# The Mamba layer's engines run in the written order, with more states between the steps of a unit's preparation and closing; D x joins TensorE's sum; two norms in a row take one root

## The chip, the cores and the metric

The kernel runs on one core of a Trainium2 chip. The metric is the device time of one execution in microseconds (us). Five executions of the kernel before took 4131.66 to 4149.81 us, with a median of 4142.33. One further view comes from the hardware profiler: it recorded the execution that took 4132.69 us, and every duration below that is not called a median is from that recording. Its span, from the first to the last instruction, is 4130.8 us.

The engines are TensorE (PE; its weight loads are listed apart as PEld), VectorE (DVE), ScalarE (ACT), GpSimd (POOL) and SyncE (SP), which issues the DMAs. Each works through its own list of instructions in order; an instruction that waits holds up all that stand behind it on that engine.

## The reference

The program is a stack of eight layers on 2048 rows of 128 numbers (8 sequences of 256). Each layer has the form `x = x + layernorm(layer(layernorm(x)))`. The change touches the seventh, a pair of Mamba blocks, one forward and one on the flipped sequence:

```python
xn = _layernorm(x, ln1_w, ln1_b)          # x is layernorm(x) of the stack already
x1 = _mamba(xn, m1_...)
x2 = flip(_mamba(flip(xn), m2_...))
return _layernorm(x1 + x2, ln2_w, ln2_b) + xn

def _mamba(x, ...):                        # E = 256 channels, N = 64 states, R = 8
    xp, z = split(x @ W_in.T)
    xc = silu(causal_conv(xp, 4 taps) + conv_b)
    dt_lo, B, C = split(xc @ W_xp.T)
    dt = softplus(dt_lo @ W_dt.T + dt_b)
    h = exp(dt * A) * h + (dt * xc) * B    # scan over time, per channel and state
    y = sum over states of h * C
    y = y + xc * D
    return (y * silu(z)) @ W_out.T
```

So a row is normed twice in a row ahead of the blocks: once by the stack, once by the layer. All numbers are f32. The last layer is a gated MLP; the six before are attention, convolution and expert layers.

## The kernel before

**The first six layers** are written as many small tasks. A planner in the program orders them by estimated costs, and a helper, `as_written` (line 156), ties the instructions of TensorE, VectorE, ScalarE and GpSimd to that order. The change leaves them as they are. The last two layers, `l3_attn` (line 1848) and `l3_ffn`, are not tied: there the order on each engine is chosen when the kernel is built, by a scheduler that goes by its own estimates of readiness and may move an instruction ahead of others written earlier.

**Units and states.** `l3_attn` works in eight units. A unit is one Mamba block (forward or flipped) on two sequences; units 0 and 1 belong to the first group of sequences, 2 and 3 to the second, and so on. A unit has 64 states, and the loop walks over all 512. For state n of a unit:

- `start` (line 2042) has SyncE load the row C of the state, broadcast to 128 partitions (`Cs`, L2046, five buffers), and ScalarE make `dA` = exp(dt A) (L2053, two instructions, three buffers). For even states ScalarE also makes `sT` = dtx B (L2050, four instructions, one per even state).
- `inputs` (line 2056) has TensorE put (dt x) B into PSUM: for even states by eight transposes of `sT` (L2068), for odd ones by 32 small products with `dB` (L2066). `dB` is made by GpSimd for two odd states at a time, three states ahead (`pre`, L2040).
- `scan` (line 2070): VectorE runs the recurrence over time (L2074), then GpSimd multiplies h by C into `hc` (L2076). In every eighth state VectorE makes this product itself, straight from PSUM.
- `add` (line 2078): three states later TensorE adds `hc`, transposed, into the unit's sum `ps_y` in PSUM (L2086, eight transposes).

In iteration i the program writes, in this order: `pre` of i+3, `inputs` of i-1, `start` of i, `scan` of i-1, `add` of i-4, one step of the closing of the unit before, one step of the preparation of the unit after.

**Preparation** (`prologue`, line 1909) starts at state 6 of the unit before. It is a generator; each `yield` is one state's pause. For the first unit of a group it norms x twice (`norm_steps`, line 220, once for each norm in a row), multiplies and adds the weights on GpSimd (L1916, L1917), then for all units: transposes or flips (L1924, L1926), four convolutions as 16 products (L1937) with a ScalarE copy each, the gate (L1944), Silu (L1948), the products for B, C and dt (L1953, L1956, L1967), Softplus (L1970), `dtx` on GpSimd (L1973), its transposes (L1983) and copy. DMAs turn `B` and `dtx` (`Bt`, `dtxTt`, L1906) and write C to memory (`cd`, L1962). If it has not ended by state 60 the rest is written at once.

**Closing** (`epilogue`, line 1988) starts at state 3 of the unit after: ScalarE copies the sum (`yT`, L1992), TensorE transposes it back (L1997), VectorE adds D x (L2001, two instructions), GpSimd multiplies by silu(z) (L2003), TensorE multiplies by W_out (L2009), ScalarE copies (L2012). After the second unit of a group the flip (L2019), the sum of both blocks (L2022), a norm, three GpSimd instructions (L2024 to L2028), a second norm and the addition to x (L2033) follow.

**A norm in steps** (`norm_steps`) is: VectorE statistics (L227, L228), GpSimd a sum and a power -0.5 (L230, L231), then four states later a small VectorE multiply (L234), one state later four ScalarE instructions (L237).

PSUM: three slots of two banks are shared by the inputs of all states (`ps_h`) and every product of preparation and closing (`ps_a`); `ps_y` has its own. A slot is free again when all readers of its tile are done.

Of the kernel before, what the change touches and what calls it, by code (L numbers as in the profile page):

```python
# [17 lines left out]
P = 128  # L18
# [154 lines left out]
class Ctx:  # L173
# [46 lines left out]
    def norm_steps(self, dst, src, n):  # L220
# [9 lines left out]
        nc.gpsimd.tensor_scalar(rs, mv[:, :, 1], EPS, None, ALU.add)  # L230
        nc.gpsimd.tensor_tensor(rs, rs, self.mhalf.to_broadcast([P, n]), ALU.pow)  # L231
        for i in range(4):
            yield
        nc.vector.scalar_tensor_tensor(mv[:, :, 0], mv[:, :, 0], -1.0, rs, ALU.mult, ALU.mult)  # L234
        yield
# [1612 lines left out]
def l3_attn(k):  # L1848
# [17 lines left out]
    with ExitStack() as es:  # L1866
# [10 lines left out]
        for m, w in enumerate(k.l3a):  # L1877
# [8 lines left out]
            nc.vector.tensor_scalar(w["A"], w["A"], 1e-20, -1.0, ALU.max, ALU.mult)  # L1886
        xTs, CLs = [], []
# [21 lines left out]
        def prologue(u, o):  # L1909
            g, m = divmod(u, 2)  # L1910
            w = k.l3a[m]
            if m == 0:
                xs = xns[g] = s2.tile([P, 4, D], F32, name="xn")
                yield from k.norm_steps(xs, k.x[:, 4 * g:4 * g + 4, :], 4)
                yield from k.norm_steps(xs, xs, 4)
                nc.gpsimd.tensor_tensor(xs, xs, over(k.l3a_ln[:, 0, :], 4, 1), ALU.mult)  # L1916
                nc.gpsimd.tensor_tensor(xs, xs, over(k.l3a_ln[:, 1, :], 4, 1), ALU.add)  # L1917
                yield
            xT, CL = xTs[u % 2], CLs[u % 2]
            ps = pb()  # L1920
            for j in range(4):
                d = slice(j * P, (j + 1) * P)
                if m == 0:
                    nc.tensor.transpose(ps[:, 0, d], xns[g][:, j, :], k.ident)  # L1924
                else:
                    nc.tensor.matmul(ps[:, 0, d], xns[g][:, j ^ 1, :], k.flip, start=True, stop=True)  # L1926
            yield
# [5 lines left out]
            for ec in range(2):  # L1933
                for b in range(2):
# [3 lines left out]
                    yield  # L1938
                    nc.scalar.activation(xc[:, ec, b * L:(b + 1) * L], ps[:, 0, 0:L], AF.Identity, bias=w["cols"][:, ec, 0:1])
                    yield  # L1940
                    yield
            for ec in range(2):
                ps = pb()
                nc.tensor.matmul(ps[:, 0, :], w["win"][:, 256 + ec * P:256 + (ec + 1) * P], xT[:, :, 3:3 + L], start=True, stop=True)  # L1944
                yield
# [11 lines left out]
            yield  # L1957
            B = s2.tile([P, 4, N], F32, name="B")
# [10 lines left out]
            yield  # L1969
            nc.scalar.activation(dt, ps, AF.Softplus)  # L1970
# [6 lines left out]
            yield  # L1977
            dtxT = s2.tile([P, 4, 2, P], F32, name="dtxT")
            ps = pb()
            for j in range(4):  # L1980
                for ec in range(2):
                    n = 2 * j + ec
                    nc.tensor.transpose(ps[:, n // 4, n % 4 * P:(n % 4 + 1) * P], dtx[:, ec, j * P:(j + 1) * P], k.ident)  # L1983
            yield
# [3 lines left out]
        def epilogue(u, o):  # L1988
# [4 lines left out]
            yield  # L1993
            py = pb()
# [3 lines left out]
            yield  # L1998
            t = s2.tile([P, 2, U], F32, name="t", tag="sp_u")
            for ec in range(2):  # L2000
                nc.vector.scalar_tensor_tensor(t[:, ec, :], o["xc"][:, ec, :], w["cols"][:, ec, 2:3], py[:, ec, :], ALU.mult, ALU.add)  # L2001
            yield
            nc.gpsimd.tensor_tensor(t, o["sz"], t, ALU.mult)  # L2003
# [236 lines left out]
```

## Time and profile before

| what | value |
|---|---|
| median of five executions | 4142.33 us |
| the profiled execution | 4132.69 us |
| its span | 4130.8 us |
| first scan of the Mamba layer begins | 2695.46 us |
| last product of its loop ends | 4045.9 us |
| VectorE busy from 2690 to 4046 | 1229.39 of 1356 us |
| GpSimd busy in it | 1241.29 us |
| ScalarE busy in it | 1197.18 us |
| TensorE busy in it | 1186.36 us, granted clock 0.98 |
| one scan (L2074) | 2266 ns x448, 2275 ns x64 |
| one hc on GpSimd, on VectorE (L2076) | 2371 ns, 1224 ns |
| one dB (L2040) | 1062 ns |
| one dA, one sT instruction | 715 ns, 495 ns |

An instruction's recorded time overlaps its neighbour's by a little, so a row of equal instructions takes less than their sum: seven scans in a row take 15.34 us. A busy share is an average over stages; which engine sets the pace has to be read stage by stage. A wait is put down to the event that came last.

### The profile page before, as it was taken

The page shows a single profiled execution, that of the slowest core. Times are in us where ns is not written, and L with a number is a line of the kernel's source. Part 1 is how long each engine was busy: PE and PEld are TensorE (multiplying, and loading weights), DVE is VectorE, ACT ScalarE, POOL GpSimd, SP SyncE. Part 2 cuts the span into 40 slices and gives each one's busy share as a digit, 9 for nine tenths or more (in the row PEclk, how much of TensorE's full clock was granted, in tenths as well). Part 3 has the DMA queues.
Part 4 walks back from the last instruction along what each step waited for, and adds up shares of the span by engine and source line. Part 5 has one row for each costly group of instructions (what it writes and reads, how often), then busy time and mean ns, then how long its engine had stood idle before and what let it go on. Part 6 is the DMA issues. An engine that isn't in the chain of part 4 may idle for free. (4 is left out here: it accounts for less than half of the span.)

```text
span 4130.8 us, 125166 instructions
## 1 busy us (share of the span) xinstructions
PE 3574.2 (87%) x55265; PEld 2808.5 (68%) x55265; DVE 3020.0 (73%) x4217; ACT 2525.5 (61%) x4465; POOL 2642.0 (64%) x1991
## 2 busy tenths in 40 slices
PE   6989988999888888999889998688988988898886
PEld 4777777777776565656555555377877876777774
DVE  7677677776755756645575568379979988998995
ACT  4455544545544545545454444299979988998993
POOL 5667667566854544332332333489989988998993
PEclk8999999999999999999999898799999999999997
DMA  1000000000001000000000000033323333443430
GB/s 58 3 3 2 3 2 3 3 2 9 2 19 38 1 1 12 25 12 11 1 1 1 6 1 1 13 110 111 112 80 115 109 106 90 110 111 91 116 114 25
DMA packets 98677, 168.89 MB, mean 41 GB/s; under 512 B 16699, under 2 KB 26582, under 8 KB 98006
## 3 DMA queue, kind: packets, MB, share of 16 engines
q1 hardware_dynamic: 98134, 160.89, 13.7%
q8 instruction: 434, 7.11, 0.7%
q14 instruction: 109, 0.89, 0.1%
HBM read 153.51 MB, written 2.10 MB: 38 GB/s over the span
## 5 line engine op out<-in xcount | busy, mean ns | idle before, releaser
L2076 POOL TENSOR_TENSOR hc<-h,Cs 128x1024 f32<-128x1024 f32 x448 | 1049.5, 2371 | 97.2 <-DVE h L2074 85.2
L2074 DVE TENSOR_TENSOR_SCAN h<-dA,ps_h 128x1024 f32<-128x1024 f32 x448 | 988.9, 2266 | 89.9 <-PE ps_h L2068 53.6
L2053 ACT ACTIVATE dA<-dt,A 128x512 f32<-128x512 f32 x1024 | 684.5, 715 | 125.4 <-DVE h L2074 92.6
L2086 PE MATMUL ps_y<-w_c_ident,hc 128*128 128x128 f32 x4096 | 561.9, 281 | 118.6 <-POOL hc L2076 85.9
L2086 PEld LDWEIGHTS ps_y<-w_c_ident,hc 128*128 128x128 f32 x4096 | 454.3, 143 | 173.1 <-POOL hc L2076 157.4
L2050 ACT ACTIVATE sT<-dtxT,B 128x256 f32<-128x256 f32 x1024 | 449.8, 495 | 3.9 <-PE ps_h L2068 3.9
L590 DVE SCALAR_TENSOR_TENSOR acc<-ps,w_l0a_conv,acc 128x254 f32<-128x254 f32 (+2 forms) x768 | 309.5, 470 | 30.6 <-ACT acc L584 30.4
L2066 PE MATMUL ps_h<-dB,dtxTt 64*64 64x64 f32 x16384 | 301.7, 223 | 19.4 <-DVE h L2074 10.1
L2066 PEld LDWEIGHTS ps_h<-dB,dtxTt 64*64 64x64 f32 x16384 | 265.9, 136 | 73.1 <-issue 46.9
L2068 PE MATMUL ps_h<-w_c_ident,sT 128*128 128x128 f32 x2048 | 276.5, 279 | 19.4 <-DVE h L2074 16.9
L2068 PEld LDWEIGHTS ps_h<-w_c_ident,sT 128*128 128x128 f32 x2048 | 239.6, 145 | 31.5 <-DVE h L2074 23.6
L742 POOL TENSOR_TENSOR Ps<-M,w_c_levels 128x512 f32<-128x512 f32 x192 | 241.9, 1275 | 5.0 <-DVE M L716 4.1
L359 ACT COPY XY<-ps 128x1024 f32<-128x1024 f32 (+1 forms) x128 | 120.5, 945 | 178.0 <-PE ps L807 164.5
L800 PE MATMUL ps<-Z,XY 64*64 64x64 f32 x4608 | 173.4, 226 | 36.0 <-DVE Z L784 25.2
L230 POOL TENSOR_SCALAR ln_rs<-ln_mv 128x4 f32<-128x4 f32 (+1 forms) x84 | 22.0, 262 | 280.2 <-DVE ln_mv L228 253.2
L800 PEld LDWEIGHTS ps<-Z,XY 64*64 64x64 f32 x4608 | 144.4, 137 | 53.2 <-DVE Z L784 27.0
L807 PE MATMUL ps<-XY,Z 64*64 64x64 f32 x5120 | 173.2, 225 | 4.4 <-issue 4.2
L784 DVE TENSOR_TENSOR Z<-ps,w_c_ident 128x512 f32<-128x512 f32 x160 | 108.0, 685 | 71.8 <-PE ps L781 71.0
L1633 ACT ACTIVATE e<-ps,nm 128x256 f32<-128x256 f32 x256 | 99.9, 484 | 99.2 <-DVE nm L1630 83.7
L351 PE MATMUL ps<-ident 128*128 128x512 bf16 x401 | 111.0, 429 | 55.2 <-DVE qn L1077 11.5
L807 PEld LDWEIGHTS ps<-XY,Z 64*64 64x64 f32 x5120 | 151.8, 138 | 7.1 <-issue 7.0
L2074 DVE TENSOR_TENSOR_SCAN ps_h<-dA,ps_h 128x1024 f32<-128x1024 f32 x64 | 145.6, 2275 | 14.8 <-PE ps_h L2066 14.5
(451 smaller groups left out, 8533.7 us busy)
## 6 DMA issues: line engine op xcount, KB each, us to landing
Cs<-cd SPq DMA_DIRECT2D x512, 256.0 KB, 3.3
dtxTt<-dtxT SPq DMA_DIRECT2D x32, 128.0 KB, 3.9
wk<-in_l0a_w SPq DMA_DIRECT2D x8, 256.0 KB, 5.7
w_h<-in_l1f_h SPq DMA_DIRECT2D x4, 512.0 KB, 3.9
w_l2a<-in_l2a_w SPq DMA_DIRECT2D x3, 512.0 KB, 4.1
w_l0a_wg<-in_l0a_wg SPq DMA_DIRECT2D x1, 1024.0 KB
w_qk<-in_l0f_wqkv SPq DMA_DIRECT2D x2, 512.0 KB, 3.9
cv<-in_l3a_m_conv SPq DMA_DIRECT2D x2, 512.0 KB, 5.1
```

Of the source, the lines that this page charges most:

```text
L359: self.nc.scalar.copy(out, in_)
L590: nc.vector.scalar_tensor_tensor(acc[:, n, s:L], p4[:, n, 0:L - s], conv[:, h2, 4 * j + n, 3 - s:4 - s], acc[:, n, s:L], ALU.mult, ALU.add,)
L742: nc.gpsimd.tensor_tensor(t, M[:, :, 0:64], over(k.l0a_levels[:, n, :], 8, 1), ALU.mult)
L800: nc.tensor.matmul(ps[own, a, at(j)], XY[rows, t, at(i)], Z[rows, za, at(zj)], start=True, stop=True)
L807: nc.tensor.matmul(ps[to, a, at(4 + j)], Z[rows, za, at(zj)], XY[rows, t, at(i)], start=True, stop=True)
L2050: nc.scalar.mul(st["s"][:, j], o["dtxT"][:, j], o["B"][:, j, n:n + 1])
L2053: nc.scalar.activation(dA[:, :, ec, :], by_seq(o["dt"][:, ec, :]), AF.Exp, scale=w["A"][:, ec, n:n + 1])
L2066: nc.tensor.matmul(ps[q, b, ec, j * 64:(j + 1) * 64], o["dtxTt"][rows, j, ec, q], dB[rows, j, :], start=True, stop=True)
L2068: nc.tensor.transpose(ps[:, j // 2, ec, j % 2 * P:(j % 2 + 1) * P], st["s"][:, j, ec, :], k.ident)
L2074: nc.vector.tensor_tensor_scan(h.rearrange(flat), st["dA"].rearrange(flat), st["in"].rearrange(flat), 0.0, ALU.mult, ALU.add)
L2076: (nc.vector if on_v else nc.gpsimd).tensor_tensor(st["hc"], h, over(by_seq(st["C"]), 2, 2), ALU.mult)
L2086: nc.tensor.matmul(o["py"][:, 2 * b + j, ec, :], st["hc"][:, b, ec, j * P:(j + 1) * P], k.ident, start=first, stop=n == N - 1, is_transpos ...
```

## The change

- `l3_attn` is wrapped in `as_written` for the four compute engines. SyncE's DMAs are not in it.
- The preparation and the closing get more `yield`s: two states instead of one between a TensorE product and the instruction that takes it out of PSUM, three between VectorE's product t and the output product, four between the layer's norm and its transposes, four instead of two behind `dtx`. `norm_steps` takes the number of pauses as a parameter; this layer uses three ahead of the small multiply and three behind it.
- The two norms in a row become one: the second's variance is v / (v + EPS), so that both together have the root of (1 + EPS) v + EPS².
- D x is summed by TensorE: a diagonal matrix D (128 x 128 per half of the channels) is made ahead of the loop, and eight products of `xc` with it open the sum `ps_y`. The VectorE instructions of L2001 go; the product with silu(z) moves from GpSimd to VectorE, one instruction reading PSUM.

```diff
-    def norm_steps(self, dst, src, n):
+    def norm_steps(self, dst, src, n, twice=False, steps=(4, 1)):
...
-        nc.gpsimd.tensor_scalar(rs, mv[:, :, 1], EPS, None, ALU.add)
+        if twice:
+            nc.gpsimd.tensor_scalar(rs, mv[:, :, 1], 1.0 + EPS, EPS * EPS, ALU.mult, ALU.add)
+        else:
+            nc.gpsimd.tensor_scalar(rs, mv[:, :, 1], EPS, None, ALU.add)
         nc.gpsimd.tensor_tensor(rs, rs, self.mhalf.to_broadcast([P, n]), ALU.pow)
-        for i in range(4):
+        for i in range(steps[0]):
             yield
         nc.vector.scalar_tensor_tensor(mv[:, :, 0], mv[:, :, 0], -1.0, rs, ALU.mult, ALU.mult)
-        yield
+        for i in range(steps[1]):
+            yield
...
+            w["D"] = s1.tile([P, 2, P], F32, name="D", bufs=2)
+            for ec in range(2):
+                nc.vector.tensor_scalar(w["D"][:, ec, :], k.ident, w["cols"][:, ec, 2:3], None, ALU.mult)
...
-                yield from k.norm_steps(xs, k.x[:, 4 * g:4 * g + 4, :], 4)
-                yield from k.norm_steps(xs, xs, 4)
+                yield from k.norm_steps(xs, k.x[:, 4 * g:4 * g + 4, :], 4, True, (3, 3))
                 nc.gpsimd.tensor_tensor(xs, xs, over(k.l3a_ln[:, 0, :], 4, 1), ALU.mult)
                 nc.gpsimd.tensor_tensor(xs, xs, over(k.l3a_ln[:, 1, :], 4, 1), ALU.add)
-                yield
+                for _ in range(4):
+                    yield
...
                         nc.tensor.matmul(ps[:, 0, 0:L], w["wk"][:, tap, ec * P:(ec + 1) * P], xT[:, b, tap:tap + L], start=tap == 0, stop=tap == 3)
                     yield
+                    yield
                     nc.scalar.activation(xc[:, ec, b * L:(b + 1) * L], ps[:, 0, 0:L], AF.Identity, bias=w["cols"][:, ec, 0:1])
                     yield
-                    yield
...
             t = s2.tile([P, 2, U], F32, name="t", tag="sp_u")
-            for ec in range(2):
-                nc.vector.scalar_tensor_tensor(t[:, ec, :], o["xc"][:, ec, :], w["cols"][:, ec, 2:3], py[:, ec, :], ALU.mult, ALU.add)
-            yield
-            nc.gpsimd.tensor_tensor(t, o["sz"], t, ALU.mult)
+            nc.vector.tensor_tensor(t, py, o["sz"], ALU.mult)
+            yield
             yield
             yield
...
-            yield from k.norm_steps(xs, xs, 4)
+            yield from k.norm_steps(xs, xs, 4, steps=(3, 3))
...
-            yield from k.norm_steps(yn, xs, 4)
+            yield from k.norm_steps(yn, xs, 4, steps=(3, 3))
...
             if n == 0:
                 o["py"] = psumy.tile([P, 4, 2, P], F32, name="ps_y")
+                for j in range(4):
+                    for ec in range(2):
+                        nc.tensor.matmul(
+                            o["py"][:, j, ec, :], o["xc"][:, ec, j * P:(j + 1) * P], w["D"][:, ec, :],
+                            start=j % 2 == ec == 0, stop=False, skip_group_check=True,
+                        )
...
-                layer(k)
+                with as_written(tc, COMPUTE if layer is l3_attn else ()):
+                    layer(k)
```

Not shown are the further single `yield`s added behind the other products (the transposes, the gate, B and C, dt, `dtx`, yT, the output product, the flip).

## The prediction

> **What bounds the kernel now.** I read the page's engine totals first, then the mean by stretch, then VectorE's waits over the Mamba layer, and last the timeline where those waits are longest. Columns of the stretches: length, then busy us (instructions) of TensorE, its weight loads, VectorE, ScalarE, GpSimd, then granted clock, DMA share, GB/s.
>
> ```profile
> PE 3574.2 (87%) x55265; PEld 2808.5 (68%) x55265; DVE 3020.0 (73%) x4217; ACT 2525.5 (61%) x4465; POOL 2642.0 (64%) x1991
> 2720.00:2780.00 60.00, 57.36 (x1037) 49.45 (x1035) 52.26 (x25) 57.98 (x106) 53.27 (x27) 1.00 0.36 102
> 3140.00:3200.00 60.00, 51.63 (x1124) 45.70 (x1113) 59.90 (x30) 55.03 (x104) 59.01 (x30) 1.00 0.39 115
> 3040.00:3100.00 60.00, 45.66 (x674) 39.69 (x673) 39.80 (x54) 39.95 (x81) 43.34 (x30) 0.86 0.21 62
> ```
>
> The totals hide three regimes. Where a unit only walks through its states (second stretch) VectorE is busy 59.9 of 60 us: it sets the pace and GpSimd is one step behind. Where the next unit is prepared (first) TensorE and ScalarE are full. Where a group ends (third) nobody is full: a third of the time is waiting.
>
> ```profile
> 2998.03 2.27 DVE L2074 TENSOR_TENSOR_SCAN ps_h<-dA,ps_h 128x1024 f32<-128x1024 f32 x1
> 3003.84 7.03 POOL L2076 TENSOR_TENSOR hc<-h,Cs 128x1024 f32<-128x1024 f32 x3 [0.34 <-DVE h L2074]
> 3010.83 1.05 POOL L2040 TENSOR_TENSOR dB<-w_c_ident,Bt 128x512 f32<-128x512 f32 x1
> 3011.85 9.35 POOL L2076 TENSOR_TENSOR hc<-h,Cs 128x1024 f32<-128x1024 f32 x4
> 3016.74 2.27 DVE L2074 TENSOR_TENSOR_SCAN ps_h<-dA,ps_h 128x1024 f32<-128x1024 f32 x1
> ```
>
> Eight states take 3016.74 - 2998.03 = 18.71 us, 2.339 each; GpSimd idles 0.34 of it. 512 states at this pace are 1197.4 us. Counting scans along the timeline, the eight units begin at 2695.46, 2856.91, 3020.19, 3206.25, 3368.95, 3555.78, 3718.53 and 3893.59, and the last product ends at 4045.9. Over 64 x 2.339 = 149.7 they lose 11.8, 13.6, 36.4, 13.0, 37.2, 13.1, 25.4 and 2.6: 153 us. What the change can win in the layer lies in these.
>
> ```profile
> DVE h L2074 <- PE ps_h L2068: 53.6, 17, 35.8
> DVE ln_mv L234 <- POOL ln_rs L231: 30.4, 10, 3.7
> DVE ln_st L227 <- POOL x L2028: 13.3, 3, 4.4
> DVE t L2001 <- PE ps_a L1997: 6.2, 7, 1.7
> 3055.75 0.16 DVE L234 SCALAR_TENSOR_TENSOR ln_mv<-ln_mv,ln_rs 128x4 f32<-128x4 f32 x1 [3.07 <-POOL ln_rs L231]
> 3062.55 0.29 DVE L227 BATCH_NORM_STATS2 ln_st<-x 128x6 f32<-128x128 f32 x1 [4.44 <-POOL x L2028]
> 3075.30 1.22 DVE L234 SCALAR_TENSOR_TENSOR ln_mv<-ln_mv,ln_rs 128x4 f32<-128x4 f32 x1 [3.72 <-POOL ln_rs L231]
> ```
>
> In the group's end VectorE stands at an instruction of a norm whose input GpSimd has not reached, with the next scan queued behind; without that scan GpSimd, ScalarE and TensorE stop too. (35.8 of the first line is the start of the layer.)
>
> **The change, part by part.**
>
> *Order and spacing.* The layer's four engines now run in the order written. The state loop's own order barely moves; the steps between do. Norm steps get three to four states between engines, and in the built order four or five scans stand between a norm's statistics and the small multiply that needs GpSimd's root. GpSimd may be 5.4 us behind the scan (hc 6 below) plus 1.3 for the root: 6.7 against three scans of 2.19, 6.6. So the waits of 30.4 and 13.3 go, nearly whole. What is late next are the sums. In units 2, 4, 6 (which carry a group's end and the next preparation) between states 4 and 24 TensorE gets D x 1.95, yT 1.0, output product 1.95, flip 1.06, xT 1.06, four convolutions of 1.9 and two gates of 0.95: 16.5 us beside 1.93 per state (3033.82 to 3037.49 and on, four groups in 3.86 for two states). Its room is 20 x (2.34 - 1.93) = 8.2, so 8.3 is lost, which also covers VectorE's own 3.5 (t, sum, statistics). From 24 to 39 ScalarE gets a copy 0.57, Silu 1.9 with two table loads of 1.28, 4.5, two copies 0.9, Softplus with two loads 3.6, a norm 1.65, a copy 1.0: 12.2, against 2.175 per state (3008.15 to 3012.50 for two), room 16 x 0.165 = 2.6 and a lead of 1.4: 8.2. Together 16.5 instead of 36.4, 37.2, 25.4: -49.5. The bounds of this term: 12 per unit as in unit 0, where no group ends (-63); and half of it if the waits only change place (-25).
>
> Units 1, 3, 5 now hold the next group's norm, which stood in units 2 and 4 and before the loop: VectorE 1.5, GpSimd a root 1.27 and two products 2.5 against room of 0.3 per eight states, 2.3 net of VectorE's; preparation as before 8.1; unit head 2.5. Sum 14.4, I take 14 against 13.2: +2.4. Units 0 and 7 stay.
>
> *D x by TensorE.* Two VectorE instructions of 0.7 (L2001) and one of GpSimd of 2.34 (L2003) become one VectorE product, 1.22 by the nearest row (hc<-ps_h, also one input from PSUM). New are eight f32 products ahead of the unit's first sum, priced as the eight of L2009: 1.95. They stand behind the copy of yT, which ends about 6 us into the unit: 6.05 + 1.95 + sum 0.93 + inputs 1.04 + 0.1 = 10.05 against 8.76 when scan 4 is due: 1.3 lost, plus the product 1.2: the 2.5 above, where before 2.6 and 3.2 were lost (t's wait of 6.2 in all goes). Bounds: nothing if yT comes early, 3.3 if the eight run at half clock as the eight at the layer's end did (3.78). Four instructions to make each D stand before the loop.
> The row on the clock: after TensorE's 2.27 us wait for yT at 2861.9 the next eight took 1.91, after 2.30 at 3211 they took 1.04. The Trainium skill (TensorE: Matmul & The Clock Gate, Part 1) says the array falls to half only after an idle window of about 3.4 us. By that rule none of these waits would slow the eight, and the sum would be the same as mine; the first row differs from it. By the first row they cost 1.9 more in each of seven units, 13 us; by the second nothing. I take the second, as the wait ahead of them is shorter here, and keep the first for the range.
>
> *One root.* Four statistics pairs, two GpSimd instructions, one small multiply and four ScalarE instructions go, per group. In the loop that is inside the sums above.
>
> *Start.* VectorE's order now puts the two weight products, which wait for cv, two A and four D instructions ahead of the first norm; before, that norm ran meanwhile. 2652.07 - 0.9 (four statistics no longer between the last expert norm's) + 2 x 1.2 + 6 x 0.26 = 2655.1; then statistics 1.3, root 1.5, multiply 0.2, ScalarE 1.7, two products 2.6: 2662.6, where the transposes began at 2658.03: +4.6. The Exp table (1.28), loaded before while ScalarE idled, now stands behind sT: +1.2. Bounds 1 to 8.
> *End.* 1.40 + 2.34 + 0.1 become 1.25: -2.6.
> *Queues.* SP is not in the fixed order. cd, four Bt and four dtxTt of a unit stand 3 to 11 Cs loads later; a preparation of the longest kind ends at state 51 of 64, so dtxTt has 13 x 2.34 = 30 us to land (3.9). Nothing. Cs behind a cd that waits for its copy have 9.5 - 3.3 = 6 us to spare. GpSimd's dB moves from behind the third and seventh hc to behind the first and fifth; hc 5 then ends at 18.42 (2.36 + 6 x 2.34 + 2 x 1.02) instead of 17.4 after scan 0 begins, and hc 6 at 20.76, 5.4 after its scan. Sum 0.99, inputs 1.16 and 0.1 follow: 20.67, and scan 9 is due at 20.90. It fits by 0.23; +1 for all, bounds 0 and 10.
> *Longer held PSUM.* Three slots serve the inputs and all other products; the latter are now held two states. One held leaves two for inputs: enough. Nothing in ordinary places; bound 1.1 (one group of inputs) per held product.
>
> Sum: -49.5 + 2.4 + 4.6 + 1.2 - 2.6 + 1 = -43. The profiled execution took 4132.7 (span 4130.8 and 1.9 around it): 4089.7. It lies 9.6 below the median of the five runs, 4142.3; at the same distance, 4099.
>
> **The rivals.**
> *Preparation also gets cheaper (0.13).* For: it is stretched over 33 states instead of some 25, and ScalarE's room grows by 8 x 0.165 = 1.3, TensorE's by 3.3. Against: ScalarE's burst of 10 us stays together. At 3 per unit and seven units: 4078.
> *Half of the gain stays away (0.08).* Norms no longer stall VectorE, but TensorE and GpSimd do: 4121.
> *The held slots decide, slower (0.11).* For: where yT's transposes or a flip overlap a preparation, two of three slots are taken and inputs start only when the scan before ends: 1.04 + 0.1 naked. Against: that holds in three places of three units, 10 us, and other waits cover most. Each preparation and epilogue holds some 12 products; over seven units they eat 43 us at 0.5 each, where it is even, 55 at 0.66, where it is slower by 0.3%; at the full 1.14 they cost 96: 4195.
> *No change to be told (0.08).* The same at 0.5, or dB's chain longer by 0.8: 64 x 0.6 = 38: 4137.
>
> **How the numbers follow.** The likeliest has 0.60, with 4078 to 4117 its own range (-63 and -25 in the first term). A measurement here tells 0.3%, 12 us: below 4130 is faster. Faster 0.60 + 0.13 + 0.08 = 0.81, same 0.08, slower 0.11. The range goes from 4065 (the cheaper preparation with the better bound) to 4145, leaving the slower case and a little below outside.
>
> **What would show it.** Right: waits for ln_rs and for x gone from VectorE's list; units 2, 4, 6 at 163 to 170 us; cadence still 18.7; GpSimd without t; TensorE's eight products at 1.95; first scan some 6 us later from cv's issue. Wrong: a cadence over 19 (dB), inputs waiting for a scan's slot throughout a preparation, or VectorE waiting at the norm's multiply as before.

## The result and the profile after

The changed kernel took 4129.36 us, the median of 34 executions (4117.76 to 4145.96). The kernel before, timed with it, took 4135.43 (62 executions, 4119.59 to 4154.78). The ratio is 0.9988, with a 95% interval of 0.9979 to 0.9997. So it gained about 5 us by the ratio (6 by the medians), where 43 were forecast. That lies within the 0.3% that the prediction called no change. The profiled execution took 4130.75 (span 4129.0).

Below are the totals and three stretches of the changed kernel: preparation in unit 0, a plain walk, and a group's end. Columns are as in the prediction.

```profile
PE 3590.5 (87%) x55393; PEld 2819.3 (68%) x55393; DVE 3022.4 (73%) x4177; ACT 2498.6 (61%) x4449; POOL 2617.2 (63%) x1975
2730.00:2790.00 60.00, 58.90 (x1103) 50.57 (x1101) 53.90 (x27) 55.67 (x101) 52.91 (x27) 1.00 0.38 105
3150.00:3205.00 55.00, 47.35 (x1008) 41.91 (x1009) 54.90 (x28) 48.91 (x95) 53.26 (x27) 1.00 0.41 123
3057.00:3117.00 60.00, 56.25 (x972) 48.74 (x971) 54.99 (x43) 51.13 (x97) 51.19 (x28) 1.00 0.32 93
```

The third line is what the change was about. In the group's end VectorE is now busy 55.0 of 60 us, where it was 39.8; TensorE is busy 56.3, where it was 45.7. VectorE's list of waits over the layer says the same (total, times, longest):

```profile
DVE h L2092 <- ACT dA L2071: 44.7, 7, 41.5
DVE h L2092 <- PE ps_h L2086: 34.0, 24, 4.1
DVE h L2092 <- PE ps_h L2084: 27.6, 21, 2.6
DVE ps_h L2092 <- PE ps_h L2084: 15.3, 8, 4.3
DVE h L2092 <- POOL hc L2094: 13.5, 12, 2.4
DVE h L2092 <- ACT sT L2068: 5.0, 5, 1.2
```

The waits for the root and for x are gone, and so is that for t. The 41.5 of the first line is the layer's start. What stands there now are waits for TensorE's inputs. They come to 76.9 us (34.0 + 27.6 + 15.3), where before they came to 50.3 without the start: 17.8 (the 53.6 of the prediction's list less 35.8), and these two:

```profile
DVE h L2074 <- PE ps_h L2066: 18.0, 15, 3.2
DVE ps_h L2074 <- PE ps_h L2066: 14.5, 6, 3.4
```

The plain walk keeps its pace. From one scan into PSUM to the next, eight states later, it is 3168.69 - 3149.99 = 18.70 us:

```profile
3149.99 2.27 DVE L2092 TENSOR_TENSOR_SCAN ps_h<-dA,ps_h 128x1024 f32<-128x1024 f32 x1
...
3168.69 2.27 DVE L2092 TENSOR_TENSOR_SCAN ps_h<-dA,ps_h 128x1024 f32<-128x1024 f32 x1
```

The ledger of the prediction can therefore be drawn up again. The loss is the loop's length, from the first scan to the end of VectorE's last product with C, minus 1197.4 us. The start is counted from the issue of the DMA of cv to the first scan, because the six layers ahead differ between executions by more than this change moves (cv was issued between 2637.70 and 2660.82 us in the runs below).

| us | before | after | forecast for after |
|---|---|---|---|
| start, cv to first scan | 47.8 | 52.6 | +5.8 |
| unit 0 | 11.8 | 12.6 | 12 |
| units 1, 3, 5, each | 13.6, 13.0, 13.1 | 19.5, 19.5, 19.6 | 14 |
| units 2, 4, 6, each | 36.4, 37.2, 25.4 | 22.4 each | 16.5 |
| unit 7 | 2.6 | 3.1 | 2.6 |
| loop's loss | 153.0 | 141.6 | |
| loop's end to span's end | 84.9 | 84.0 | -2.6 |

Loop, start and end make -11.4 + 4.8 - 0.9 = -7.5 us. Two terms failed. Units 2, 4 and 6 gained 31.8 instead of 49.5, and units 1, 3 and 5 lost 19.0 instead of 2.4. Each is some 17 us off, and together they are nearly all of the missing gain. The experiments show that they failed for different reasons.

Below, an eight is a run of eight states of a unit (the first is 0 to 7); what it loses is its length from scan to scan minus 18.71 us.

### The profile page after: what moved, and what is told of

It reads as the page before. It is cut to its first block, busy times and chain, and to the rows that moved or that the text cites. A ratio compares the mean times of both kernels' runs of the same rounds, so it can differ in the third digit from the quotient of the medians.

```text
span 4129.0 us, 125478 instructions
## 1 busy us (share of the span) xinstructions
PE 3590.5 (87%) x55393; PEld 2819.3 (68%) x55393; DVE 3022.4 (73%) x4177; ACT 2498.6 (61%) x4449; POOL 2617.2 (63%) x1975
## 3 DMA queue, kind: packets, MB, share of 16 engines
q1 hardware_dynamic: 98134, 160.89, 13.7%
## 4 chain that ended last, share of the span: by engine, by line
PE 43%; POOL 19%; DVE 18%; issue 12%; ACT 7%; DMA 0%; POOLq 0%; DVEq 0%; ACTq 0%; SPq 0%
POOL hc L2094 12%; PE ps L1523 3%; PE ps L583 2%; DVE acc L595 2%; POOL dB L2058 2%; DVE h L2092 2%; PE ps L805 1%; PE ps L812 1%; PE ps L859 1%; DVE nm L1635 1%; PE ps L919 1%; PE ps L786 1%; PE ps L1379 1%; ACT dA L2071 1%; PE ps L894 1%
## 5 line engine op out<-in xcount | busy, mean ns | idle before, releaser
L2071 ACT ACTIVATE dA<-dt,A 128x512 f32<-128x512 f32 x1024 | 675.0, 712 | 150.9 <-DVE h L2092 144.2
L2068 ACT ACTIVATE sT<-dtxT,B 128x256 f32<-128x256 f32 x1024 | 433.9, 495 | 0.0
L2084 PEld LDWEIGHTS ps_h<-dB,dtxTt 64*64 64x64 f32 x16384 | 264.0, 135 | 60.7 <-issue 36.4
L2086 PE MATMUL ps_h<-w_c_ident,sT 128*128 128x128 f32 x2048 | 274.4, 277 | 13.6 <-DVE h L2092 7.9
L234 POOL TENSOR_SCALAR ln_rs<-ln_mv 128x4 f32<-128x4 f32 (+1 forms) x76 | 19.3, 255 | 296.1 <-DVE ln_mv L229 269.0
L2092 DVE TENSOR_TENSOR_SCAN ps_h<-dA,ps_h 128x1024 f32<-128x1024 f32 x64 | 145.6, 2275 | 15.3 <-PE ps_h L2084 15.3
```

Of the source, the lines that this page charges most:

```text
L2068: nc.scalar.mul(st["s"][:, j], o["dtxT"][:, j], o["B"][:, j, n:n + 1])
L2071: nc.scalar.activation(dA[:, :, ec, :], by_seq(o["dt"][:, ec, :]), AF.Exp, scale=w["A"][:, ec, n:n + 1])
L2084: nc.tensor.matmul(ps[q, b, ec, j * 64:(j + 1) * 64], o["dtxTt"][rows, j, ec, q], dB[rows, j, :], start=True, stop=True)
L2086: nc.tensor.transpose(ps[:, j // 2, ec, j % 2 * P:(j % 2 + 1) * P], st["s"][:, j, ec, :], k.ident)
L2092: nc.vector.tensor_tensor_scan(h.rearrange(flat), st["dA"].rearrange(flat), st["in"].rearrange(flat), 0.0, ALU.mult, ALU.add)
```

## The experiments

Three theories for the missing gain were set against each other:

- **L**: the loop of latency. The scan of state k must be followed by GpSimd's hc of k, TensorE's sum of k, the inputs of k+4 and the scan of k+4, since each engine works in its written order. GpSimd idles 0.34 of 18.71 us in a plain walk, so this loop has next to no slack. Any single piece of other work on GpSimd or TensorE then comes out as a wait of VectorE, even where the engine has room on average.
- **T**: throughput. One engine or another has more work in a stretch than fits, and slack in the loop cannot change that.
- **H**: the PSUM slots that are now held for two states.

All kernels compute the whole reference. The times of the first two rows and of the last are medians; every other kernel was executed once, so the comparison is by the loop's loss, for the reason just given.

| kernel | loop's loss | unit 1 | unit 2 | start | time |
|---|---|---|---|---|---|
| before | 153.0 | 13.6 | 36.4 | 47.8 | 4135.43 |
| after | 141.6 | 19.5 | 22.4 | 52.6 | 4129.36 |
| order alone | 195.4 | 31.2 | 28.0 | 55.4 | 4187.03 |
| all but the order | 136.0 | 12.2 | 29.7 | 38.9 | 4104.10 |
| after, sum later, with buffers | 109.6 | 12.5 | 20.7 | 52.1 | 4091.88 |
| after, sum later alone | 117.8 | 13.1 | 22.2 | 52.4 | 4096.59 |
| after, buffers alone | 151.3 | 21.3 | 22.9 | 52.5 | 4149.76 |
| after, dB earlier | 116.4 | 14.9 | 19.1 | 52.5 | 4096.07 |
| after, norm's products apart | 139.6 | 19.5 | 22.4 | 52.4 | 4128.93 |
| after, D x as before | 140.4 | 18.2 | 22.6 | 52.6 | 4126.31 |
| after, four dA | 137.6 | 19.8 | 20.8 | 52.4 | 4127.84 |
| after, slots held for one state | 143.2 | 21.6 | 22.0 | 52.3 | 4114.96 |
| after, small multiply in four | 138.3 | 19.3 | 20.4 | 52.1 | 4131.80 |
| combined | 86.9 | 7.8 | 18.2 | 44.8 | 4054.31 |
| combined, free order, without the edit of the start | 123.9 | 11.8 | 25.4 | 38.8 | 4091.97 |
| combined, late preparation | 78.9 | 7.9 | 15.4 | 45.1 | 4060.13 |

### The order alone, and all but the order

```diff
 # order alone: the kernel before with
-                layer(k)
+                with as_written(tc, COMPUTE if layer is l3_attn else ()):
+                    layer(k)
```

> The kernel before with its Mamba layer alone put in the written order: no added pauses, D x on VectorE, two roots. Yardstick: what the eight units lose over 18.71 us per eight states (before 153 us, the changed kernel 141.5), by unit 11.8, 13.6, 36.4, 13.0, 37.2, 13.1, 25.4, 2.6 before and 12.6, 19.5, 22.4, 19.5, 22.4, 19.6, 22.4, 3.1 after. Theory L (the loop scan, hc, sum, inputs, scan has no room: whatever GpSimd or TensorE get besides reaches VectorE): the norm in units 1, 3, 5 costs as after or more (20 to 24), the group ends about 25 to 30; sum 150 to 170. Theory P (the pauses do it, order is indifferent): units as before, about 153. Theory O (order alone removes the norm waits): units 2, 4, 6 at 22 to 25, sum 135 to 145.

```diff
 # all but the order: the changed kernel with
-                with as_written(tc, COMPUTE if layer is l3_attn else ()):
+                with as_written(tc, ()):
```

> The changed kernel without the fixed order of the Mamba layer: pauses, D x on TensorE and one root stay, the scheduler orders. Theory L: the norm work moves to where the scheduler puts it; units 2 and 4 again over 28, units 1, 3, 5 near 14; sum 135 to 155. Theory P: as the changed kernel, 141. Theory O: norm waits of VectorE for the root are back, some 20 us or more in its list of waits, sum about 150.

The written order alone costs 42.4 us in the loop (195.4 against 153.0) and 7.6 at the start. In the written order the spacing and the other edits win 53.8 (195.4 to 141.6). Left to the scheduler they win 17.0 (153.0 to 136.0) and 8.9 at the start. So two large effects stand behind the small result: the written order takes away what the scheduler had arranged, and the spacing pays it back. With all the other edits in place the written order still costs 5.6 in the loop (141.6 against 136.0) and 13.7 at the start. None of the three expectations had the order alone as dear as it is: units 1, 3 and 5 lose 31, where theory L said 20 to 24. With the order alone, unit 1 shows it:

```profile
2884.44 3.78 PE L2009 MATMUL ps_a<-w_l3a_m_wout,t 128*128 128x128 f32 x16 [4.52 <-POOL t L2003]
...
2889.96 2.29 DVE L2074 TENSOR_TENSOR_SCAN h<-dA,ps_h 128x1024 f32<-128x1024 f32 x1 [4.19 <-PE ps_h L2068]
```

TensorE stands 4.52 us at the output product, whose t GpSimd has not made, and 4.19 of it reach VectorE. In the free order with all other edits the old stall is still there in unit 2: VectorE has put a norm's statistics ahead of the scans and stands at them.

```profile
3060.56 0.49 DVE L228 BATCH_NORM_STATS2 ln_st<-x 128x6 f32<-128x128 f32 x2 [6.42 <-POOL x L2045]
```

### Slack in the loop

```diff
-            if i >= 4:
-                v, c = divmod(i - 4, N)
+            if i >= 5:
+                v, c = divmod(i - 5, N)
 # one more turn of the loop; hc 5 buffers, Cs 6 instead of 4 and 5;
 # with buffers: also h 4 instead of 3, sT 2 instead of 3
```

> The changed kernel with the sum of state k written one state later (behind the inputs of k+4 instead of ahead of them), and one buffer more for h, hc and C, one less for sT. No work is added or taken away. Theory L: hc may then be late by 2.2 us more before VectorE feels it, so the loss falls from 141.5 to 80 to 110, and TensorE's waits for hc lose their followers. Theory T (TensorE and ScalarE are simply full while a unit is prepared, 16.5 and 12 us beyond their room): at most 10 us less, 132 or more. Theory H (slots of PSUM held two states longer): unchanged, as the slots are the same.

> Of the run with the sum a state later, only the sum's place (five hc and six Cs, which it needs); h keeps three buffers and sT one. Theory L: the state of slack between GpSimd's product and the sum is what won 32.0 of loop time there; here the loop loses 110 to 120. If the buffers of h and sT did it, the loop loses 135 to 142, as in the changed kernel.

> The other half of that run: h in four buffers, sT in two, the sum where the changed kernel has it. Theory L: VectorE's waits for a free h (13.5) and for sT (5.0) go, and most of what is behind them stays late on TensorE: the loop loses 130 to 140. If the buffers did it, it loses 110 to 118.

TensorE adds hc one state later, and no work changes. The loop loses 117.8 instead of 141.6 with the later sum alone, and 109.6 with the buffers too. The buffers alone win nothing, where 130 to 140 was expected: 151.3, or 148 when this run's pace of 18.76 us for eight states, against 18.71 in the others, is taken out (3.2 us over 64 eights). So the slack won 23.8 of the 32.0, and the buffers are worth something only behind it. The buffers are a mixed edit: h gets a fourth, but sT has three in the changed kernel and two here (two of the expectations have this the wrong way round). Alone, VectorE's waits for a free h fell from 13.5 to 8.2 and those for sT rose from 5.0 to 9.4, so a fourth h by itself was not measured.

Where the slack won matters as much. With the later sum alone units 1, 3 and 5 fell from 19.5 to 13.1 each, 19 us of the 23.8, and unit 0 from 12.6 to 9.2. Units 2, 4 and 6 stayed at 22.2. So theory L accounts for units 0, 1, 3 and 5, and not for 2, 4 and 6. What limits units 2, 4 and 6 can be read off two eights of unit 2 in the changed kernel, the second and the fourth:

```profile
3060.74:3084.75 24.01, 23.60 (x462) 21.86 (x463) 21.13 (x20) 18.36 (x37) 19.67 (x11) 1.00 0.34 92
3105.50:3130.32 24.82, 22.69 (x404) 18.56 (x394) 22.02 (x19) 24.70 (x40) 23.34 (x15) 1.00 0.39 101
```

In the second TensorE (the first busy column) works 23.60 of 24.01 us at full granted clock; in the fourth ScalarE (the fourth busy column) works 24.70 of 24.82. There an engine has more work than fits into the eight, as theory T says. With the later sum these eights lose 7.1 and 6.4, where 5.3 and 6.1 were lost.

What the slack meets in the other units can be read off TensorE's queue. This is unit 1 of the changed kernel, where GpSimd makes the next group's two norm products:

```profile
2910.03 1.31 POOL L1923 TENSOR_TENSOR xn<-xn,w_l3a_ln 128x512 f32<-128x512 f32 x1
2911.42 1.27 POOL L1924 TENSOR_TENSOR xn<-xn,w_l3a_ln 128x512 f32<-128x512 f32 x1
2912.65 4.67 POOL L2094 TENSOR_TENSOR hc<-h,Cs 128x1024 f32<-128x1024 f32 x2
2915.05 1.79 PE L2109 MATMUL ps_y<-w_c_ident,hc 128*128 128x128 f32 x8 [2.71 <-POOL hc L2094]
2916.64 1.06 PE L1932 MATMUL ps_a<-w_c_ident,xn 128*128 128x128 f32 x4
2917.49 1.64 PE L2086 MATMUL ps_h<-w_c_ident,sT 128*128 128x128 f32 x8
2919.26 6.64 DVE L2092 TENSOR_TENSOR_SCAN h<-dA,ps_h 128x1024 f32<-128x1024 f32 x3 [4.10 <-PE ps_h L2086]
```

The two products come in front of an hc. TensorE waits 2.71 us for that hc, and behind it stand the transposes of the preparation and the inputs. VectorE waits 4.10. The same place with the later sum:

```profile
2895.11 1.27 POOL L1923 TENSOR_TENSOR xn<-xn,w_l3a_ln 128x512 f32<-128x512 f32 x1
2895.76 9.00 DVE L2092 TENSOR_TENSOR_SCAN h<-dA,ps_h 128x1024 f32<-128x1024 f32 x4
2896.47 1.27 POOL L1924 TENSOR_TENSOR xn<-xn,w_l3a_ln 128x512 f32<-128x512 f32 x1
2897.79 0.66 PE L1932 MATMUL ps_a<-w_c_ident,xn 128*128 128x128 f32 x4 [1.49 <-POOL xn L1924]
2898.28 1.04 PE L2086 MATMUL ps_h<-w_c_ident,sT 128*128 128x128 f32 x8
```

The products are as long, but VectorE runs four scans without a gap. The second such piece is dtx in the preparation, followed at once by a dB: 3.5 us in which no hc is made. Here it is in unit 2 of the changed kernel:

```profile
3134.99 2.37 POOL L1985 TENSOR_TENSOR dtx<-dt,xz 128x1024 f32<-128x1024 f32 x1
...
3137.48 1.06 POOL L2058 TENSOR_TENSOR dB<-w_c_ident,Bt 128x512 f32<-128x512 f32 x1
3138.49 4.67 POOL L2094 TENSOR_TENSOR hc<-h,Cs 128x1024 f32<-128x1024 f32 x2
...
3140.90 1.97 PE L2109 MATMUL ps_y<-w_c_ident,hc 128*128 128x128 f32 x8 [3.70 <-POOL hc L2094]
```

In the loop of the changed kernel TensorE waits ten times for 2.7 to 3.7 us at a sum, always behind these two pieces (units 1, 3, 5 at both, units 0, 2, 4, 6 at dtx). With the later sum no wait of TensorE in the loop reaches 1.8. The lists of waits, changed kernel first, then the later sum alone:

```profile
PE ps_y L2109 <- POOL hc L2094: 106.8, 114, 3.7
```

```profile
PE ps_y L2109 <- POOL hc L2094: 64.8, 114, 1.2
```

### dB two states earlier

```diff
-            if i + 3 < units * N:
-                pre(made[(i + 3) // N], (i + 3) % N)
+            if i + 5 < units * N:
+                pre(made[(i + 5) // N], (i + 5) % N)
 # and five states, not three, ahead of the loop
```

> The changed kernel with dB made five states ahead instead of three, so that GpSimd makes it behind the third and seventh hc as before and not behind the first and fifth. No work is added. The cadence stays 18.71 by all theories. Theory L: hc 1, 2, 5 and 6 end 1.0 us earlier, so each insertion on TensorE beside them costs up to 1 us less: the loss falls by 10 to 25 us, to 117 to 131. Theories T and H: within 4 us of 141.5.

It wins 25.2 us of loop (116.4), more than the bound of 10 that the prediction gave for dB's place. The plain stretches lose nothing either way. The gain lies in the eights where something else is already late.

### The norm's two products apart

```diff
                 nc.gpsimd.tensor_tensor(xs, xs, over(k.l3a_ln[:, 0, :], 4, 1), ALU.mult)
+                for _ in range(4):
+                    yield
                 nc.gpsimd.tensor_tensor(xs, xs, over(k.l3a_ln[:, 1, :], 4, 1), ALU.add)
```

> Four states stand between GpSimd's two products of the next group's norm, which the changed kernel writes one behind the other (2.6 us in a row). Theory L (the loop scan, GpSimd's product, sum, inputs, scan has no room, so whatever stands on GpSimd in one piece comes out at VectorE): the third eight states of units 1, 3 and 5 lose 3 to 4 us instead of 5.25, the loop 135 to 138 instead of 141.6. Theory T (throughput of GpSimd over eight states): the same 2.6 us is only moved, part of it into the next eight states, and the loop stays at 141 to 142. Theory H (held PSUM slots): nothing changes.

The third eight of unit 1 fell from 5.25 to 1.7, more than theory L said, and TensorE's waits of 2.7 are gone. But unit 1 stayed at 19.5, because the later steps of the preparation moved four states back and lost what was won (3.65, 0.78, 3.92 and 4.41 in the eights behind, where 1.62, 4.4, 1.3 and 1.95 had stood). Theory L explains the place and not the total: 139.6 lies between its 135 to 138 and the 141 to 142 of theory T. In the combined version, which has slack, the same eights of unit 1 lose 0.0, 2.0, 0.2, 2.5 and 0.

### D x as before

```diff
-            nc.vector.tensor_tensor(t, py, o["sz"], ALU.mult)
+            for ec in range(2):
+                nc.vector.scalar_tensor_tensor(t[:, ec, :], o["xc"][:, ec, :], w["cols"][:, ec, 2:3], py[:, ec, :], ALU.mult, ALU.add)
+            yield
+            nc.gpsimd.tensor_tensor(t, o["sz"], t, ALU.mult)
 # and no eight products with D ahead of the first sum
```

> D x is taken back to VectorE and GpSimd as in the kernel before, the rest is the changed kernel. Theory L: the first eight states of units 1 to 6 lose 2.7 to 3.3 us instead of 4.5 to 4.7, since TensorE's 1.95 no longer stand ahead of the first sum; the second eight of units 1, 3 and 5 lose 2 to 3 instead of 0.3, since GpSimd's product of 2.3 us stands in the loop again; together 141 +- 4, that is, D by TensorE is worth next to nothing. Theory T with TensorE as the limit: 1.9 us per unit are won and none is given back, 128 to 130.

The unit's first eight falls to 3.4, and later ones give it back: in units 1, 3 and 5 the second loses 1.1 to 2.6 instead of 0.3 and the seventh 3.5 instead of 1.95. The loop loses 140.4. So D x by TensorE is worth nothing here that can be told.

### A fourth dA; slots held for one state

```diff
-            dA = st["dA"] = s3.tile([P, 2, 2, L], F32, name="dA")
+            dA = st["dA"] = s3.tile([P, 2, 2, L], F32, name="dA", bufs=4)
```

> ScalarE may run one more state ahead (four dA buffers instead of three). If the waits for dA and ScalarE's bursts carry the losses of the fourth and fifth eight states, the 4.4 of units 1, 3 and 5 and the 6.1 of units 2, 4 and 6 fall to 2 to 4, the loop to 120 to 128. If these losses are the loop over GpSimd and TensorE too (theory L), less than 1 us per unit changes: 136 to 141.

```diff
                     yield
-                    yield
                     nc.scalar.activation(xc[:, ec, b * L:(b + 1) * L], ps[:, 0, 0:L], AF.Identity, bias=w["cols"][:, ec, 0:1])
                     yield
+                    yield
 # likewise at five other products
```

> The products of the preparation and of the group's end are evacuated one state after TensorE made them, as in the kernel before, and the state that this saves stands behind the evacuation: the spread stays, only the PSUM slot is held for one state less. Theory H (held slots eat the gain): some 12 products per preparation and epilogue at 0.5 to 1.1 us each, the loop loses 20 us or more less, 100 to 122 instead of 141.6. Theory L: slots are not what is waited for, 141 +- 4.

Both leave the loop within 4 us of where it was (137.6 and 143.2). The fourth dA did lower the eights that it was meant for (the fifth of units 1, 3 and 5 from 4.4 to 3.3, the fourth of units 2 and 4 from 6.1 to 4.1), but later eights gave that back, so ScalarE's lead is not what the gain went to. Theory H falls as well, for ten of the thirteen products of a preparation and a closing: those for B and C, the transposes of dtx and those of yT were still held for two states.

### The small multiply of a norm

VectorE's idle time in the loop fell from 121.1 to 102.1 us, but its busy time rose from 1229.4 to 1236.9. One instruction on 128x4 grew by about as much, 7.2. The groups of instructions in the loop, before and after (busy, mean ns, idle ahead):

```profile
L234 DVE SCALAR_TENSOR_TENSOR ln_mv<-ln_mv,ln_rs 128x4 f32<-128x4 f32 x10 | 3.8, 377 | 30.4 <-POOL ln_rs L231 30.4
```

```profile
L238 DVE SCALAR_TENSOR_TENSOR ln_mv<-ln_mv,ln_rs 128x4 f32<-128x4 f32 x9 | 11.0, 1218 | 0.0
```

Each of the nine ends with a GpSimd instruction, to some 0.03 us. In the rows below the four hc begin 2.34 apart, so the first ends at 3092.8, and the multiply at 3092.84:

```profile
3090.44 9.37 POOL L2094 TENSOR_TENSOR hc<-h,Cs 128x1024 f32<-128x1024 f32 x4
3091.30 1.54 DVE L238 SCALAR_TENSOR_TENSOR ln_mv<-ln_mv,ln_rs 128x4 f32<-128x4 f32 x1
```

```diff
-        nc.vector.scalar_tensor_tensor(mv[:, :, 0], mv[:, :, 0], -1.0, rs, ALU.mult, ALU.mult)
+            for i in range(n):
+                nc.vector.tensor_scalar(mv[:, i, 0:1], mv[:, i, 0:1], rs[:, i:i + 1], -1.0, ALU.mult, ALU.mult)
 # in this layer's norms only
```

> In the changed kernel the nine small multiplies of the Mamba layer's norms on 128x4 (L238) took 11.0 us in the loop, 1.22 each, where they took 0.16 when GpSimd was idle; each of the nine ended within 0.03 us of the end of GpSimd's instruction. Here each is four instructions on 128x1 with the root as a scalar per partition, so that only one tensor is read from SBUF. If VectorE waits for GpSimd because of the second SBUF input (theory P), the four take 0.3 to 0.7 together, whatever GpSimd does, VectorE's busy time in the loop falls by 5 to 8, and the loop loses 134 to 140 instead of 141.6. If it waits for GpSimd's instruction for another reason, their sum stays at 1.2 or more, and the loop at 141 to 143.

With one tensor from SBUF the four take 0.55 us together, in the middle of GpSimd's work:

```profile
3094.93 7.04 POOL L2098 TENSOR_TENSOR hc<-h,Cs 128x1024 f32<-128x1024 f32 x3
3095.77 0.55 DVE L240 TENSOR_SCALAR ln_mv<-ln_mv,ln_rs 128x1 f32<-128x1 f32 x4
```

VectorE's busy time in the loop fell by 5.4, and the loop loses 138.3, 3.3 less. So some of the 7 was on the path, but less than all; at 3.3 the split is not sharp. In the version with late preparation it brought nothing:

> The same edit in the combined version with the late preparation, where the nine took 1.3 us each on average. Theory P: the loop loses 66 to 74 instead of 78.9, the time is about 0.980 of the kernel before. Otherwise it is as that version, 0.982.

The loop's loss was 81.0 against 78.9, where 66 to 74 was expected, and the ratio to the kernel before is 0.9819 (0.9798 to 0.9840).

### Together

```diff
 # sum later (hc 5 buffers, h 4, sT 2; Cs stays at 5), dB two states earlier, the norm's products apart, dA 4, and at the start:
-        for _ in prologue(0, made[0]):
-            pass
+        first = prologue(0, made[0])
+        for _ in range(12):
+            next(first)
+        for w in k.l3a:
+            made_weights(w)
+        for _ in first:
+            pass
```

`made_weights` holds the products with cv, A and D, which now stand behind the first norm.

> The steps that theory L asks for, together: the sum a state later with a fifth hc, a fourth h and a second sT, dB two states earlier, the two products of the norm apart, four dA buffers, and at the start the first norm ahead of the weight products. Theory L: the loop loses 75 to 95 us instead of 141.6, the first scan stands 42 to 45 us after the issue of cv instead of 52.6, the time is 4055 to 4078. Theory T: at most the 109.6 of the sum alone, less 3, and the time is 4080 to 4090.

> The combined version (without the edit of the start) with the layer's order left to the scheduler as in the kernel before. If the slack in the loop is what counts in either order (theory L), it wins here as it did in the written order: the loop loses 100 to 120 instead of the 136.0 of the free order alone, the first scan stands 38 to 41 us after cv's issue, the time is 4065 to 4090. The waits at the norm's instructions stay in the second eight states of units 2, 4 and 6 (15 to 18 us each), so it does not reach the combined version in written order. If the slack is only worth something in the written order, the loop loses 130 to 136.

The combined version loses 86.9 in the loop and starts 7.8 us sooner, inside what theory L said and below the 106.6 that theory T allowed. In the free order, without the edit of the start, it loses 123.9: the slack is worth something there too, but less than expected. What remains in units 2, 4 and 6 was theory T's. In the second eight of unit 2, which loses 7.1, TensorE works 24.76 of 25.81 us:

```profile
3021.54:3047.35 25.81, 24.76 (x470) 22.76 (x470) 21.38 (x19) 20.24 (x40) 18.82 (x10) 1.00 0.33 102
```

So the preparation was moved away from the group's end there:

```diff
-                if n == 6 and u + 1 < units:
+                if n == (14 if u in (2, 4, 6) else 6) and u + 1 < units:
```

> The combined version, and in units 2, 4 and 6 the preparation starts at state 14 instead of 6. In the second eight states there TensorE was busy 24.7 of 25.9 us: eight sums and inputs 15.4, output product 1.95, flip 1.06, four convolutions 7.6 make 26.0 against 18.71, and 7.1 were lost. If TensorE's throughput is the limit in this stretch, the loss falls to 0 to 1 there and returns in part in the third eight (7.6 + 15.4 = 23.0 against 18.71, 4.3 instead of 2.06): units 2, 4 and 6 lose 13 to 16 instead of 18.2, the loop 73 to 80 instead of 86.9. If the loss is the loop's latency at the group's end, it stays at 7 in the second eight and nothing is won: 85 to 90.

> The combined version with the late preparation, timed against the kernel before. By the layer's parts it gains 153.0 - 78.7 = 74 in the loop, 47.8 - 45.2 = 2.6 at the start and about 1 at the end: 78, ratio 0.981, if the other layers take the same time. By theory T it cannot be below the 109.6 of the later sum alone, that is not below 0.988.

The second eight lost 3.8 instead of 7.1 (0 to 1 was expected) and the third stayed at 2.05 (4.3 was expected); the fifth rose from 0 to 2.0. Units 2, 4 and 6 fell from 18.2 to between 15.4 and 15.9 each. The loop's loss was 78.7 in the first run and 78.9 in the one timed. That version beats both kernels: 4060.13 us, the median of five executions (4052.71 to 4066.63), against 4136.27 for the kernel before on the same chip. The ratio is 0.9821, with an interval of 0.9795 to 0.9847.

## Why the prediction was wrong

- **The pace and the norm's waits**: right. Eight states take 18.70, and the waits of 30.4, 13.3 and 6.2 are gone.
- **Units 2, 4, 6 at 16.5**: the first step that failed. "What are late next are the sums" was right, and the price was not. The step added up TensorE's work from state 4 to 24 and ScalarE's from 24 to 39 and took off the room that they have there on average, 8.2 us and 2.6. But the work falls into single eights. The measured 22.4 are 4.5, 5.3, 2.0, 6.1 and 4.4 in the first five; in the second TensorE is full and in the fourth ScalarE, as shown above, while in the fifth TensorE works 16.6 of 23.1. Room in one eight was not room for the work of another. One more state of distance did not change that (22.2); starting the preparation later did, from 18.2 to 15.4 in the combined version. How the rest of the 22.4 divides is open; dB two states earlier took 3.3 of it.
- **Units 1, 3, 5 at 14**: the second step that failed. It too set GpSimd's pieces against the average room of an eight and took the preparation over "as before". The dB paragraph had worked out that a plain stretch fits by 0.23 us, and this lack of slack was used for dB alone. The 19.5 are the unit's head at 4.7 (2.5 in the sum), the norm's two products with what stands behind them at 5.3 (3.8 with all the norm), and a preparation at 9.3 (8.1). GpSimd's dtx of 2.4 us, with a dB behind it, has no term of its own, and seven of TensorE's ten long waits stand behind it. A state of slack, with no work taken away, brought these units back to 13.1.
- **dB "fits by 0.23", bounds 0 and 10**: right in plain stretches, wrong where anything else is late. Two states earlier are worth 25.2, and the bound was 10.
- **The wait at the norm's multiply goes**: it went, but the multiply itself then took 11.0 us instead of 3.8. The slow form stood in the prediction's own fence (1.22 us at 3075.30, beside 0.16 at 3055.75) and was not read.
- **D x**: right in kind. The eight products took 2.05 (1.95 forecast), and scan 4 came 1.16 late (1.3):

```profile
2874.32 2.05 PE L2102 MATMUL ps_y<-D,xz 128*128 128x128 f32 x16
...
2878.25 2.29 DVE L2092 TENSOR_TENSOR_SCAN h<-dA,ps_h 128x1024 f32<-128x1024 f32 x1 [1.16 <-PE ps_h L2086]
```

- **The start**: +4.8 against +5.8. The products with cv do stand ahead of the first norm, as the rows below show; counted from cv the transposes begin 5.2 later than before (4.6 forecast). Of the 1.2 for the Exp table nothing is seen in the sum. The small multiply behind the root begins at 2664.34 and the transposes at 2668.91. Putting the norm first takes 7.8 off.

```profile
2657.82 1.23 DVE L1888 TENSOR_TENSOR wk<-cv,w_l3a_m_win 128x1024 f32<-128x1024 f32 x1 [7.45 <-DMA cv<-in_l3a_m_conv]
2664.34 0.16 DVE L238 SCALAR_TENSOR_TENSOR ln_mv<-ln_mv,ln_rs 128x4 f32<-128x4 f32 x1 [1.50 <-POOL ln_rs L235]
2668.91 1.12 PE L1932 MATMUL ps_a<-w_c_ident,xn 128*128 128x128 f32 x4 [26.61 <-POOL xn L1924]
```

- **The end**: -0.9 instead of -2.6. Why is open; in the runs whose last instructions are those of the changed kernel (sum later, later alone, buffers alone, dB earlier, products apart, four dA) this stretch came to 82.5 to 86.0, so one execution of each kernel does not tell 1.7.
- **Held PSUM costs nothing**: right for the ten products that were tried, by the run with slots held for one state.
- **The rivals**: "half of the gain stays away" named the mechanism that comes nearest, TensorE and GpSimd stalling in VectorE's place, though not ScalarE. It had 0.08 and priced the loss at half the gain, where most of it went.
- **The chances**: 0.81 stood on faster by over 0.3%, and the time, though inside the wide range, fell within 0.3%. The likeliest case's own range does not follow from its bounds either: -63 and -25 in the first term give 4086 and 4124, not 4078 and 4117, and the time lies above both. What spoke for this case in the prediction, at 0.08, were the held slots and dB; the runs show it by another way, the two steps above.

The sum of the parts came nearer than the parts. With the later sum and its buffers the loop lost 109.6, and the forecast's units add up to 106; but units 2, 4 and 6 still lost 20.7 instead of 16.5, and unit 0 only 7.4 instead of 12. So the near agreement of the sums is luck in part.

What stays open: the run with the norm's products apart shows that moving one piece away does not win its whole price when the steps behind it move as well. That TensorE and ScalarE are full in units 2, 4 and 6 is read from the trace, and only TensorE's share was tried by moving work (the late preparation).

## What to carry to other kernels

Where engines run behind each other in a fixed order, ask first how many steps of slack lie between a result and the step that takes it. With none, a single piece of other work can come out as a wait on the next engine whatever the average room, so price each piece on each engine, the almost full one above all. Then add up each engine's work in short stretches, here eight states, and not over a whole phase: where one stretch holds more than fits, slack does not help, and the work has to be moved. One more step of distance, with the buffers for it, may be worth more than removing the work. An order by hand and a wider spacing should be tried apart, since here one took 42 us in the loop and the other gave 54 back.

## What was not expected of the hardware

A VectorE instruction on 128x4 with two SBUF inputs took 0.16 us while GpSimd was idle and, in the changed kernel, 0.37 to 1.75 while it worked, each time up to the end of GpSimd's instruction. With one such input, 0.55 for four. The Trainium skill (SBUF — State Buffer, Who interferes with whom) says that a VectorE instruction with two SBUF inputs contends with a GpSimd instruction that reads SBUF, and calls the port pair that they share an exclusive lock. The nine rows agree with it.

The length of a TensorE wait did not tell whether the clock falls. In the changed kernel the sum of eight transposes, 1.04 to 1.09 us at full clock, took 1.79, 1.72 and 1.68 behind waits of 2.7, 1.09 behind all three of 3.32 to 3.34, and 1.97 behind all four of 3.56 to 3.70. The granted clock was 0.58 in the first of these sums (2915.05 to 2916.64), 1.00 behind the first wait of 3.32, and 0.50 behind the 3.70 shown above. With slots held for one state the sum took 1.97 behind the three waits of 3.34 to 3.35, 1.09 behind three of 3.70 and 1.97 behind one of 3.71, and behind the three of 2.71 once 1.61 and twice 1.09. The Trainium skill (TensorE: Matmul & The Clock Gate, Part 1) speaks of a free-running window of about 3.4 us. A window that runs free could give such a scatter, though no run here shows the window itself. The slow sums behind 2.7 us do not fit a fall that needs a whole idle window of 3.4.
